# Last batch handed from experts to routing on chip, the experts' deadline moved by 19 turns, and expert places counted by running sums

## The chip, the cores and the metric

The kernel runs on one core of a Trainium2 chip. A core has five engines with a queue of instructions each: TensorE (PE; its weight loads are listed as PEld), VectorE (DVE), ScalarE (ACT), GpSimd (POOL) and SyncE (SP), which here issues nearly all the ordinary DMAs; GpSimd issues the indirect ones. The metric is the device time of one execution in microseconds; the number compared is the median of several runs.

## What is computed

The reference is two transformer layers over 16 batches of 512 tokens with 128 features, all in float32. Cut to what matters here:

```
xn = layernorm(x)
x  = x + memory_scan(xn) + L0(xn)       # L0: conv, attention, layernorm, 8 dense experts, layernorm
xn = layernorm(x)
x  = x + L1_attention(xn) + L1_experts(xn)

# end of L0, after the dense experts
x1 = x1 + moe_out;  L0 = layernorm(x1) * g2 + b2n

# L1_attention: causal attention, a convolution, causal attention again, a projection
# L1_experts: 32 experts, the best 8 for each token, at most 128 tokens for each expert
logits = xn @ gate.T;  top 8;  softmax weights
pos  = cumsum(one_hot(expert), axis=0) - 1        # place of a token in its expert's buffer
buf  = zeros(E, 128, H).at[expert, pos].set(xn)   # places from 128 on are dropped
eo   = (silu(buf @ gate_w) * (buf @ up_w)) @ down_w
out  = sum over the token's 8 experts of eo[expert, pos] * weight
```

The cumulative sum runs over all tokens of all batches, so no expert's list of tokens is known before the last batch has been routed.

## The kernel before

**Turns.** The program is a set of Python generators (stages), and the class Turns steps each of them once in a turn, in order of a priority number. What a stage emits between two yields lands in the engines' queues in that place. TensorE's order is exactly the order written; 1275 turns make the program. A stage can wait for a mark that another has set (after), for some turns (idle) or for a free PSUM bank (room).

**What runs in them.** For each batch of layer 0: front0, tops and back (attention), post0, then ffn (the 8 dense experts: 32 pieces, each one first, the matmul pair phe, and one second, the four calls into pye; the result of an expert is scaled by ScalarE into y and added to ac by GpSimd, L618). For each batch of layer 1: middle (layernorm after the experts, residual sum into acc, layernorm, router, and a table ctab of running counts inside each tile of 128 tokens), front1, tops and back twice with between, and last. Layer-1 batches start 44 turns apart (TBB) from turn 480 (t0). tops writes scores s and takes their row maxima on VectorE (L395, or L402 and L403); these go through DRAM back into rows of qx (top, L420 and L424); back computes s again, exp on ScalarE into e (L475), masks the diagonal block on GpSimd (L483), or on VectorE once the gathers are over (L481), and multiplies with the values into pc.

**How the dense experts are spread.** ffn takes in each turn as many pieces as a credit allows; the credit grows by due(b, left), which spreads all pieces still to do evenly over the turns up to pools["until"]. At the end of each turn fill adds a dummy matmul (L206) when the turn holds little work for TensorE and no dense-expert piece was handed out in the last turns.

**The last batch.** ffn stores its result ac to DRAM (x1d); middle loads it two idle turns ahead of its use, computes both layernorms (VectorE the moments, GpSimd the rest), stores the transposed xT to DRAM (xt), and front1 loads it again and waits three turns.

**Places.** route (here the end of middle) copies, for each tile of 128 tokens, each expert's total into a column of totT by a DMA of 0.1 KB (L1235). When the last batch is routed and all weight tiles lent from the pool mid are read, the stage moe begins. It loads the mask memE, makes running sums of the 64 columns of totT in six doubling steps on VectorE (L1337, L1338), spreads them over partitions by four matmuls pt (512 columns each, from a masked product bd), and finds for each expert and place the tile (istar) and the place in it (base). 32 indirect gathers gt from ctab (L1375) and counts lt (L1369) give the tokens. Then 16 pairs of experts follow, three turns apart: gather the tokens xg (L1413), transpose (tpx), pgu, peo, and scatter-add eo into acc in DRAM (L1458). At the end total adds what attention left in ao for the last batches and writes out (L1485, L1492).

Of the kernel before, what the change touches and what calls it, by code (L numbers as in the profile page):

```python
# [82 lines left out]
def network(ctx: ExitStack, tc: tile.TileContext, a, out):  # L83
# [60 lines left out]
    def mark(*m):  # L144
        done[m] = clock[0]
# [375 lines left out]
    credit, fetched = [0.0], {}  # L521
# [24 lines left out]
    def ffn(b):  # L546
# [99 lines left out]
        nc.sync.dma_start(x1d[0, b], flat(ac))  # L646
# [536 lines left out]

    def middle(mid, b):

        yield from after(("ffn", b))
# [20 lines left out]
        yield from idle(2)  # L1207
        yield from room()
# [34 lines left out]
        mark("xw", b)  # L1243
        yield


    def front1(b):
        yield from after(("x2", b))
        got = []
        yield from take(free_values, got)  # L1250
        z = live[1, b] = {"vp": got[0]}
        xT = l1.tile([P, S], F32, tag="st", bufs=2, name="xT")
        nc.sync.dma_start(xT, xt[1, b])
        yield from idle(3)
# [74 lines left out]
    def moe(mo):  # L1329

        memE = load(mo, "mske", [EXP1, EXP1])

        cur = totT
        s_ = 1
        while s_ < NTILE:
            nxt = mo.tile([EXP1, NTILE], F32, tag=f"cum{s_}", bufs=1, name=f"cum{s_}")
            nc.vector.tensor_copy(nxt[:, 0:s_], cur[:, 0:s_])  # L1337
            nc.vector.tensor_tensor(nxt[:, s_:], cur[:, s_:], cur[:, : NTILE - s_], ALU.add)  # L1338
            cur, s_ = nxt, 2 * s_
        per = 512 // NTILE  # L1340

        def places(u):
# [3 lines left out]
            nc.vector.tensor_tensor(bd, bc(cur, 1, per), bc(memE[:, es], 2, NTILE), ALU.mult)  # L1346
            yield
# [12 lines left out]
        yield from side(*[places(u) for u in range(EXP1 // per)])  # L1360
        nc.vector.tensor_scalar(base, base, -1.0, col("iota"), ALU.mult, ALU.add)
        rowf = mo.tile([P, EXP1], F32, tag="rowf", bufs=1, name="rowf")
# [4 lines left out]
        def count(e):  # L1367
            lt = mo.tile([P, P], F32, tag="lt", name="lt")
            nc.vector.tensor_scalar(  # L1369
                lt, gts[e], base[:, e : e + 1], None, ALU.is_le, ALU.add, accum_out=tok[:, e : e + 1]  # L1370
            )

        for e in range(EXP1):
            gt = mo.tile([P, P], F32, tag="gt", bufs=12, name="gt")
            nc.gpsimd.indirect_dma_start(  # L1375
                out=gt, out_offset=None, in_=ctab,
                in_offset=bass.IndirectOffsetOnAxis(ap=rowi[:, e : e + 1], axis=0),
                bounds_check=EXP1 * NTILE - 1, oob_is_err=True,
            )
# [11 lines left out]
        gidf = mo.tile([P, EXP1], F32, tag="gidf", bufs=1, name="gidf")  # L1391
        nc.vector.tensor_scalar(gidf, tok, float(N - 1), None, ALU.min)
        gidx = mo.tile([P, EXP1], I32, tag="gidx", bufs=1, name="gidx")
        nc.vector.tensor_copy(gidx, gidf)

        inv = mo.tile([P, EXP1], F32, tag="inv", bufs=1, name="inv")
        nc.vector.tensor_scalar(inv, tok, float(N), col("iota"), ALU.is_ge, ALU.mult)
        nc.vector.scalar_tensor_tensor(inv, tok, float(N), inv, ALU.min, ALU.add)
        sidx = mo.tile([P, EXP1], I32, tag="sidx", bufs=1, name="sidx")
        nc.vector.tensor_copy(sidx, inv)  # L1400
        yield

# [94 lines left out]
    pools["until"] = t0 + (B - 1) * TBB - 10  # L1497
# [14 lines left out]
    with tc.tile_pool(name="mid", bufs=1) as mid:  # L1512
# [129 lines left out]
```

## Time and profile before

| | us |
|---|---|
| median of 3 runs | 3590.16 (3588.07 to 3597.58) |
| the profiled execution | 3586.38 |
| its span, first to last instruction | 3584.7 |
| TensorE busy | 3388.3 (95%) |
| VectorE busy | 2319.8 (65%) |
| ScalarE busy | 2217.0 (62%) |
| GpSimd busy | 1541.4 (43%) |

Times below are in us from the start of the span. Because TensorE follows the written order, each turn has a place in the trace, the start of its first matmul:

| turn | starts at | what stands there |
|---|---|---|
| 481 | 1474.0 | layer 1 begins |
| 1131 | 3201.8 | |
| 1133 | 3205.4 | last matmul of the dense experts |
| 1154 | 3252.7 | |
| 1159 | 3262.5 | transposes of the last batch's x2 (tp) |
| 1161 | 3270.0 | |
| 1169 | 3287.1 | first pt |
| 1177 | 3320.1 | first gather is issued to GpSimd's queue (it runs at 3326.5) |
| 1200 | 3379.5 | gathers are over |
| 1210 | 3402.1 | first scatter-add is issued |
| 1258 | 3548.3 | last scatter-add is issued |

A line of a view of waits reads: who waited, for whom, us in total, times, the longest. A line of a timeline has start, length, engine, line, operation, names, and in brackets the engine's idle time before it and what ended that.

### The profile page before, as it was taken

To read this page: it belongs to the slowest core of one execution; us is meant where nothing else is said; L and a number is where in the kernel's file an instruction comes from. 1 tells how busy PE (TensorE), PEld (TensorE's weight loads), DVE (VectorE), ACT (ScalarE), POOL (GpSimd) and SP (SyncE) were. 2 spreads that over 40 slices of the span, in tenths; PEclk is the share of its full clock that TensorE was granted. 3 is DMA by queue.
4 is the path that set the end of the run, shared out by engine and by line. 5 is a ranking of instruction groups with operands and counts; after the bars stand their busy time and mean duration, and the time that the engine had idled before them with its cause. 6 is when DMAs were issued, how large, how long until landed. Compare 5 with 4: busy or idle time off the path is not lost.

```text
span 3584.7 us, 63937 instructions
## 1 busy us (share of the span) xinstructions
PE 3388.3 (95%) x22085; PEld 1903.2 (53%) x22085; DVE 2319.8 (65%) x6045; ACT 2217.0 (62%) x4919; POOL 1541.4 (43%) x2386
## 2 busy tenths in 40 slices
PE   6999999899999999999999999999999999998887
PEld 3445555454555455555555555555555555553444
DVE  5676666566756565556467676666666666667885
ACT  1566656665666787766656666666666666664444
POOL 5423532433531455433544444434444444433653
PEclk7999999899999999999999999999999999998997
DMA  5222222212222233334344444444344434433343
GB/s 176 70 70 71 74 72 78 67 53 85 76 73 88 89 110 108 110 118 125 106 111 136 126 121 113 121 136 122 95 132 121 134 114 111 132 106 98 92 102 91
DMA packets 289794, 370.37 MB, mean 103 GB/s; under 512 B 45984, under 2 KB 141376, under 8 KB 289088
## 3 DMA queue, kind: packets, MB, share of 16 engines
q1 hardware_dynamic: 282304, 359.46, 34.7%
q0 software_dynamic: 7168, 6.82, 1.2%
q8 instruction: 177, 2.90, 0.3%
q14 instruction: 145, 1.19, 0.1%
HBM read 236.58 MB, written 132.99 MB: 103 GB/s over the span
## 4 chain that ended last, share of the span: by engine, by line
PE 50%; DVE 4%; DMA 2%; ACT 2%; POOL 1%; issue 1%; SPq 1%; POOLq 0%; DVEq 0%; ACTq 0%
PE s L197 13%; PE pye L610 10%; PE phe L197 10%; PE pc L197 8%; PE pq L197 1%; DVE s L395 1%; PE fill L206 1%; PE tpc L251 1%; PE tp L251 1%; DVE nm L403 1%; PE po L197 1%; DVE s L402 1%; ACT e L475 1%; PE pjk L197 1%; PE pv L197 1%
## 5 line engine op out<-in xcount | busy, mean ns | idle before, releaser
L475 ACT ACTIVATE e<-s 128x512 f32<-128x512 f32 (+1 forms) x2432 | 1274.6, 576 | 556.6 <-PE s L197 514.3
L403 DVE TENSOR_REDUCE nm<-s 128x1 f32<-128x512 f32 (+2 forms) x1408 | 906.7, 682 | 512.0 <-PE s L197 510.6
L395 DVE CUSTOM_DVE_ANT_0 s<-s,sb_const 128x512 f32<-128x512 f32 (+1 forms) x1024 | 623.4, 643 | 388.2 <-PE s L197 386.6
L483 POOL TENSOR_SCALAR_AFFINE_SELECT e<-e 128x128 f32<-128x128 f32 (+2 forms) x1270 | 426.7, 344 | 746.6 <-ACT e L475 721.1
L197 PE MATMUL s<-kx,qx 64*128 64x512 f32 (+3 forms) x3072 | 624.4, 431 | 44.4 <-ACT e L475 15.4
L197 PE MATMUL pc<-e,vp 128*32 128x512 f32 (+3 forms) x6144 | 625.8, 506 | 13.4 <-POOL e L483 7.2
L610 PEld LDWEIGHTS pye<-ew,hTe 128*128 128x128 f32 x4096 | 519.8, 193 | 177.9 <-issue 157.6
L197 PEld LDWEIGHTS s<-kx,qx 64*128 64x128 f32 x3072 | 272.8, 187 | 574.4 <-issue 226.6
L610 PE MATMUL pye<-ew,hTe 128*128 128x128 f32 x4096 | 563.0, 281 | 1.5 <-ACT hTe L600 1.4
L197 PE MATMUL s<-qx,kx 64*128 64x512 f32 (+3 forms) x3072 | 536.3, 357 | 26.9 <-DVE nm L403 7.8
L197 PE MATMUL phe<-x1T,ew 128*128 128x512 f32 x1024 | 547.5, 619 | 7.0 <-DMA ew<-in_ew 3.0
L600 ACT ACTIVATE hTe<-phe,sb_cols 128x512 f32<-128x512 f32 x512 | 353.7, 691 | 240.7 <-PE phe L197 238.1
L197 PEld LDWEIGHTS s<-qx,kx 64*128 64x128 f32 x3072 | 305.7, 189 | 78.5 <-ACT e L475 20.4
L618 POOL TENSOR_TENSOR ac<-ac,y 128x512 f32<-128x512 f32 x128 | 163.7, 1279 | 422.6 <-ACT y L617 359.9
L402 DVE TENSOR_TENSOR s<-s,sb_const 128x256 f32<-128x256 f32 (+1 forms) x384 | 181.6, 515 | 190.0 <-PE s L197 157.1
L197 PEld LDWEIGHTS pc<-e,vp 128*32 128x32 f32 x6144 | 150.9, 110 | 238.9 <-issue 174.9
L197 PEld LDWEIGHTS phe<-x1T,ew 128*128 128x128 f32 x1024 | 157.9, 192 | 73.1 <-issue 43.5
L617 ACT ACTIVATE y<-pye,pr 128x128 f32<-128x128 f32 x512 | 146.8, 369 | 31.1 <-PE pye L610 26.9
L395 DVE DVE_READ_ACCUMULATOR2_ANT nm<- 128x1 f32 x1024 | 144.0, 141 | 0.0
L212 POOL TENSOR_SCALAR rs_t<-ss 128x4 f32<-128x4 f32 (+1 forms) x56 | 11.5, 206 | 228.6 <-ACT sq L265 227.3
L1458 POOL DMA_INDIRECT acc<-eo,sidx x32 | 51.6, 1612 | 74.3 <-DVE eo L1452 26.6
L212 POOL TENSOR_SCALAR rs_t<-ln_mv 128x4 f32<-128x4 f32 x64 | 12.7, 198 | 162.5 <-DVE ln_mv L222 159.7
(297 smaller groups left out, 3935.7 us busy)
## 6 DMA issues: line engine op xcount, KB each, us to landing
ew<-in_ew SPq DMA_DIRECT2D x256, 256.0 KB
kx<-rk SPq DMA_DIRECT2D x192, 256.0 KB
qx<-rq SPq DMA_DIRECT2D x128, 256.0 KB
rq<-hi SPq DMA_DIRECT2D x64, 256.0 KB
rq<-lo SPq DMA_DIRECT2D x64, 256.0 KB
rk<-hi SPq DMA_DIRECT2D x64, 256.0 KB
rk<-lo SPq DMA_DIRECT2D x64, 256.0 KB
qx<-r SPq DMA_DIRECT2D x64, 256.0 KB
```

The costliest lines, as they stand in the source:

```text
L197: nc.tensor.matmul(o, lhsT=lhsT, rhs=rhs, start=start, stop=stop)
L251: nc.tensor.transpose(tp[:, t * P : (t + 1) * P], src(t), ident)
L395: newest[0] = nc.vector.tensor_tensor_reduce(out=sv[r][:, 0, :], in0=sv[r][:, 0, :], in1=row["caus"][:, S - n :], scale=1.0, scalar=-BIG, ...
L402: nc.vector.tensor_tensor(dg, dg, bc(row["caus"][:, S - P :], 1, per), ALU.add)
L403: newest[0] = nc.vector.tensor_reduce(nm[:, qt, r, t : t + per], sv[r], AX.X, ALU.max)
L475: nc.scalar.activation(e[:, r, 0 : per * n], s[r], AF.Exp, scale=SCALE)
L483: cleared[0] = nc.gpsimd.affine_select(out=ev[:, r, :, 0:P], in_=ev[:, r, :, 0:P], pattern=[[0, per], [1, P]], compare_op=ALU.is_ge, fill= ...
L600: nc.scalar.activation(hs[i], ph, AF.Relu, bias=col("fb", i))
L610: nc.tensor.matmul(pye[0][:, t, :], lhsT=h[:, t * P : (t + 1) * P], rhs=w2[e][:, f, :], start=(f == 0 and t == 0), stop=(f == 3), skip_gro ...
L617: nc.scalar.mul(y[:, t, :], pye[0][:, t, :], pr[:, t, e : e + 1])
L618: nc.gpsimd.tensor_tensor(ac, ac, y, ALU.add)
L1458: nc.gpsimd.indirect_dma_start(out=acc, out_offset=bass.IndirectOffsetOnAxis(ap=sidx[:, e : e + 1], axis=0), in_=eo[:, i, :], in_offset=No ...
```

## The change

- The last batch's ffn keeps ac in SBUF (final["ac"]) and does not store it. A new stage part, centred, takes the place of the first half of middle for this batch. It loads the residual xa once batch 14 is routed and adds the bias on GpSimd. After the last expert it reads ac, and VectorE does centring, scaling and residual sum in two operations for each tile, and the second layernorm's normalising. xT stays in SBUF and front1 uses it without a load or idle turns.
- pools["until"] goes from 10 turns ahead of t0 + 15 x 44 to 9 turns behind it, so that due spreads the dense experts' pieces over 19 turns more.
- The running sums are made batch by batch at the end of route: three turns behind the mark xw, four small VectorE operations on the batch's four columns of totT add to the sums so far, upto. The doubling steps go, and memE is loaded early.
- moe begins as soon as the last batch's sums are marked, in the pool fb, and does not wait for the lent tiles before its pairs. Each of its four places parts has two idle turns between bd and pt, and they start two turns apart. Gather tiles gt have 10 buffers and not 12.

```diff
-        nc.sync.dma_start(x1d[0, b], flat(ac))
+        if b == B - 1:
+            final["ac"] = ac
+        else:
+            nc.sync.dma_start(x1d[0, b], flat(ac))
...
+    def centred(mid, b):
+
+        yield from after(("xw", b - 1))
+        xa = mid.tile([P, TB, D], F32, tag="st", bufs=4, name="xa")
+        nc.sync.dma_start(xa, acc_b[b])
+        yield from idle(3)
+        nc.gpsimd.tensor_tensor(xa, xa, bc(row["b2n"], 1, TB), ALU.add)
+        yield from after(("ffn", b))
+        ac = final["ac"]
...
+        yield from moments(ac, got)
+        mv, rs = got[0]
+        for t in range(TB):
+            nc.vector.scalar_tensor_tensor(
+                x2[:, t, :], ac[:, t, :], mv[:, t, 0:1], row["g2"], ALU.subtract, ALU.mult
+            )
+            nc.vector.scalar_tensor_tensor(
+                x2[:, t, :], x2[:, t, :], rs[:, t : t + 1], xa[:, t, :], ALU.mult, ALU.add
+            )
+            if t == 1:
+                yield
+        yield
+        nc.sync.dma_start(acc_b[b], x2)
+        yield from layernorm(xwt[:, :, 0:D], x2, on=(nc.vector,))
+        yield from room()
+        xT = l1.tile([P, S], F32, tag="st", bufs=2, name="xT")
+        transpose_tokens(xT, xwt[:, :, 0:D])
+        final["xT"] = xT
...
         mark("xw", b)
+        yield from idle(3)
+        of = totT[:, b * TB : (b + 1) * TB]
+        ups = sm.tile([EXP1, TB], F32, tag="ups", name="ups")
+        nc.vector.tensor_copy(ups[:, 0:1], of[:, 0:1])
+        nc.vector.tensor_tensor(ups[:, 1:], of[:, 1:], of[:, : TB - 1], ALU.add)
+        to = upto[:, b * TB : (b + 1) * TB]
+        carry = upto[:, b * TB - 1 : b * TB] if b else 0.0
+        nc.vector.tensor_scalar(to[:, 0:2], ups[:, 0:2], carry, None, ALU.add)
+        nc.vector.scalar_tensor_tensor(to[:, 2:], ups[:, 2:], carry, ups[:, 0:2], ALU.add, ALU.add)
+        mark("upto", b)
...
-        xT = l1.tile([P, S], F32, tag="st", bufs=2, name="xT")
-        nc.sync.dma_start(xT, xt[1, b])
-        yield from idle(3)
+        xT = final.pop("xT", None)
+        if xT is None:
+            xT = l1.tile([P, S], F32, tag="st", bufs=2, name="xT")
+            nc.sync.dma_start(xT, xt[1, b])
+            yield from idle(3)
...
-        memE = load(mo, "mske", [EXP1, EXP1])
-
-        cur = totT
-        s_ = 1
-        while s_ < NTILE:
-            nxt = mo.tile([EXP1, NTILE], F32, tag=f"cum{s_}", bufs=1, name=f"cum{s_}")
-            nc.vector.tensor_copy(nxt[:, 0:s_], cur[:, 0:s_])
-            nc.vector.tensor_tensor(nxt[:, s_:], cur[:, s_:], cur[:, : NTILE - s_], ALU.add)
-            cur, s_ = nxt, 2 * s_
+    upto = mw.tile([EXP1, NTILE], F32, name="upto")
+    memE = load(mw, "mske", [EXP1, EXP1])
+
+    def moe():
+
+        yield from after(("upto", B - 1))
...
-            nc.vector.tensor_tensor(bd, bc(cur, 1, per), bc(memE[:, es], 2, NTILE), ALU.mult)
-            yield
+            nc.vector.tensor_tensor(bd, bc(upto, 1, per), bc(memE[:, es], 2, NTILE), ALU.mult)
+            yield from idle(2)
...
-        yield from side(*[places(u) for u in range(EXP1 // per)])
+        yield from timed(*[(2 * u, places(u)) for u in range(EXP1 // per)])
...
-            gt = mo.tile([P, P], F32, tag="gt", bufs=12, name="gt")
+            gt = fb.tile([P, P], F32, tag="gt", bufs=10, name="gt")
...
+        while "mo" not in pools:
+            yield
+        mo = pools["mo"]
...
-    pools["until"] = t0 + (B - 1) * TBB - 10
+    pools["until"] = t0 + (B - 1) * TBB + 9
...
-        pools.update(weights=[att, fb])
+        pools.update(weights=[att, fb], work=2)
+        turns.stages.append((turns.turn, 3, moe()))
         turns.run(until=lambda: not lent)
     with tc.tile_pool(name="mo", bufs=2) as mo:
-        pools["work"] = 2
-        turns.stages.append((turns.turn, 3, moe(mo)))
+        pools["mo"] = mo
         turns.stages += [(turns.turn, 5, total(b)) for b in range(B)]
```

More of the change, by code (lines that the diff above doesn't have):

```diff
@@ L518, in conv @@
         mm(o[:, 0 : S - 1], w(2), src[:, 1:S], start=False)
-    credit, fetched = [0.0], {}
+    credit, fetched, final = [0.0], {}, {}
     def due(b, left):
@@ L1182, in network @@
     pools["pairs"] = True
+    def centred(mid, b):
[6 more added lines that the diff above has]
+        ac = final["ac"]
+        x2 = mid.tile([P, TB, D], F32, tag="st", bufs=4, name="x2")
+        xwt = mid.tile([P, TB, XW], F32, tag="xwt", bufs=1, name="xwt")
+        got = []
+        yield from moments(ac, got)
[16 more added lines that the diff above has]
+        final["xT"] = xT
+        mark("x2", b)
+        yield
+        return xT, xwt
     def middle(mid, b):
+        if b == B - 1:
+            yield from route(mid, b, *(yield from centred(mid, b)))
+            return
         yield from after(("ffn", b))
@@ L1207, in middle, with route @@
         yield from idle(2)
+        yield from route(mid, b, xT, xwt)
+    def route(mid, b, xT, xwt):
         yield from room()
@@ L1327, in network @@
     tok = mw.tile([P, EXP1], F32, name="tok")
-    def moe(mo):
-        memE = load(mo, "mske", [EXP1, EXP1])
-        cur = totT
-        s_ = 1
-        while s_ < NTILE:
-            nxt = mo.tile([EXP1, NTILE], F32, tag=f"cum{s_}", bufs=1, name=f"cum{s_}")
-            nc.vector.tensor_copy(nxt[:, 0:s_], cur[:, 0:s_])
-            nc.vector.tensor_tensor(nxt[:, s_:], cur[:, s_:], cur[:, : NTILE - s_], ALU.add)
-            cur, s_ = nxt, 2 * s_
+    upto = mw.tile([EXP1, NTILE], F32, name="upto")
+    memE = load(mw, "mske", [EXP1, EXP1])
+    def moe():
+        yield from after(("upto", B - 1))
         per = 512 // NTILE
@@ L1359, in places @@
             nc.vector.tensor_reduce(base[:, es], le, AX.X, ALU.max)
-        yield from side(*[places(u) for u in range(EXP1 // per)])
+        yield from timed(*[(2 * u, places(u)) for u in range(EXP1 // per)])
         nc.vector.tensor_scalar(base, base, -1.0, col("iota"), ALU.mult, ALU.add)
-        rowf = mo.tile([P, EXP1], F32, tag="rowf", bufs=1, name="rowf")
+        rowf = fb.tile([P, EXP1], F32, tag="rowf", bufs=1, name="rowf")
         nc.vector.scalar_tensor_tensor(rowf, istar, float(NTILE - 1), C1("eoff"), ALU.min, ALU.add)
@@ L1367, in count @@
         def count(e):
-            lt = mo.tile([P, P], F32, tag="lt", name="lt")
+            lt = fb.tile([P, P], F32, tag="lt", bufs=2, name="lt")
             nc.vector.tensor_scalar(
@@ L1390, in moe @@
         nc.vector.scalar_tensor_tensor(tok, istar, float(P), tok, ALU.mult, ALU.add)
-        gidf = mo.tile([P, EXP1], F32, tag="gidf", bufs=1, name="gidf")
+        gidf = fb.tile([P, EXP1], F32, tag="gidf", bufs=1, name="gidf")
         nc.vector.tensor_scalar(gidf, tok, float(N - 1), None, ALU.min)
-        gidx = mo.tile([P, EXP1], I32, tag="gidx", bufs=1, name="gidx")
+        gidx = fb.tile([P, EXP1], I32, tag="gidx", bufs=1, name="gidx")
         nc.vector.tensor_copy(gidx, gidf)
-        inv = mo.tile([P, EXP1], F32, tag="inv", bufs=1, name="inv")
+        inv = fb.tile([P, EXP1], F32, tag="inv", bufs=1, name="inv")
         nc.vector.tensor_scalar(inv, tok, float(N), col("iota"), ALU.is_ge, ALU.mult)
         nc.vector.scalar_tensor_tensor(inv, tok, float(N), inv, ALU.min, ALU.add)
-        sidx = mo.tile([P, EXP1], I32, tag="sidx", bufs=1, name="sidx")
+        sidx = fb.tile([P, EXP1], I32, tag="sidx", bufs=1, name="sidx")
         nc.vector.tensor_copy(sidx, inv)
         yield
+        while "mo" not in pools:
+            yield
+        mo = pools["mo"]
         def fetch(e2):
```

## The prediction

> **What bounds the kernel now.** I read the windows first, then TensorE's waits, then GpSimd's timeline at the end. Columns of a window: its length, busy us and instructions of PE, PEld, DVE, ACT and POOL, granted clock, DMA share, GB/s.
>
> ```profile
> 1800.00:3060.00 1260.00, 1244.01 (x9168) 736.38 (x9164) 846.02 (x2594) 814.37 (x1719) 562.63 (x1205) 1.00 0.42 120
> 3201.80:3252.80 51.00, 46.47 (x329) 22.32 (x325) 36.70 (x112) 27.63 (x58) 24.22 (x56) 0.97 0.39 97
> 3218.10:3260.80 42.70, 41.25 (x277) 18.50 (x276) 33.80 (x105) 22.42 (x46) 24.44 (x54) 0.98 0.26 69
> 3297.30:3326.50 29.20, 25.45 (x125) 11.65 (x125) 26.06 (x62) 10.12 (x21) 6.87 (x19) 0.70 0.36 91
> 3326.50:3379.50 53.00, 45.44 (x276) 19.17 (x274) 39.56 (x148) 22.73 (x46) 44.88 (x69) 0.94 0.41 103
> 3405.00:3555.00 150.00, 127.69 (x867) 72.43 (x866) 111.67 (x358) 72.88 (x157) 81.05 (x58) 0.85 0.38 78
> ```
>
> The first row is the long stretch in which layer-0 experts (phe, pye) share the turns with layer-1 attention: TensorE is busy 1244 of 1260 us at clock 1.00, VectorE only 846. It waits for almost nothing there; the three longest entries:
>
> ```profile
> PE phe L197 <- DMA ew<-in_ew: 3.0, 1, 3.0
> PE s L197 <- DMA qx<-top: 2.3, 5, 1.1
> PE tpc L251 <- ACT cs L448: 1.9, 4, 0.5
> ```
>
> So there a turn lasts as long as its matmuls, and a matmul taken out shortens it. After the experts end (3207) it is otherwise: dummy matmuls (fill) pad TensorE, and places that wait stand out. The largest, with the DMA behind it:
>
> ```profile
> PE pt L197 <- DVE bd L1346: 6.3, 1, 6.3
> ```
> ```profile
> 3287.11 0.56 SPq L1235 DMA_DIRECT2D totT<-ct  x1
> ...
> 3291.35 0.14 DVE L1337 COPY cum<-totT 32x1 f32<-32x1 f32 x1 [2.61 <-DMA totT<-ct]
> ```
>
> The last totT copy is issued at 3287.11, VectorE waits until 3291.35, runs twelve small cum operations, and pt starts at 3295.28. From the first gather on, GpSimd's queue sets the pace:
>
> ```profile
> 3326.54 1.34 POOL L1375 DMA_INDIRECT gt<-ctab,rowi  x1 [0.70 <-DMA acc<-xs]
> ...
> 3378.44 1.01 POOL L1375 DMA_INDIRECT gt<-ctab,rowi  x1 [0.30 <-DVE lt L1369]
> 3383.76 1.03 POOL L1413 DMA_INDIRECT xg<-xw,gidx  x1 [2.28 <-DVE gidx L1394]
> ...
> 3404.95 1.68 POOL L1458 DMA_INDIRECT acc<-eo,sidx  x1 [13.33 <-DVE eo L1452]
> ...
> 3474.31 1.57 POOL L1458 DMA_INDIRECT acc<-eo,sidx  x1 [2.45 <-DVE e L481]
> ...
> 3483.06 1.69 POOL L1458 DMA_INDIRECT acc<-eo,sidx  x1 [2.47 <-DVE nm L395]
> ...
> 3553.53 1.55 POOL L1458 DMA_INDIRECT acc<-eo,sidx  x1 [2.45 <-DVE e L481]
> ```
>
> 32 gathers fill 53 us between masks (idle 0.2 to 0.3 before each); 32 scatters follow, one after another's landing, never under 8.75 us a pair (3474.31 to 3483.06); the span ends 31.2 us after the last scatter (3584.7 - 3553.5). So first gather to end is 258.2 us of one queue, and what sets the end is how early the first gather is.
>
> **The change, by turns.** TensorE's order is written out turn by turn, so both programs can be counted; times of turns are those of their first matmul in the trace. Last expert matmul: turn 1133 before, 1151 after. First pt: 1169, then 1174. First gather: 1177, then 1183. Scatters: 1210 to 1258, then 1216 to 1262. Turns in all: 1275, then 1274. Up to turn 1131 (3201.8 us) nothing differs on TensorE but where expert pieces stand and a few small pieces of batch 14's routing.
>
> (a) **Experts taken out of turns 481 to 1130.** Twelve phe (two matmuls each) and thirteen pye groups (eight each) leave. The chain of waits has runs of them at 0.86 and 0.89 us, others at 1.05 and 1.09. 12 x 0.86 + 13 x 0.89 = 21.9, upper end 12 x 1.05 + 13 x 1.09 = 26.8. Cover: none, TensorE is full. Fitting the lengths of turns 568 to 1095 (one attention phase apart) to their expert time gives 0.96 to 1.1 us for each us taken out, 0.79 at the low end of its error: lower end 17. I take -21.9, by the packed rows.
>
> (b) **The same pieces put into turns 1131 to 1153.** These took 51.0 us, with 46.47 busy, so 4.5 idle; twelve fills worth 8.2 us by width (1.05 us for a full one) go, because their room is used. 21.9 - 8.2 - 4.5 = +9.2. At matmul pitch (0.43 us for 512 columns) instead of modelled ends the idle time is 9.5: +4 is the low end. Allowing idle time to be filled only within its own turn gives +12.
>
> (c) **Last expert to first gather.** From turn 1161 (3270.0) to the first gather: 56.5 us before, 16 turns and 6.4 us of queue. After: 22 turns. The unburdened rate is 42.70 us for 20 turns, 2.13 each: 22 x 2.13 + 6.4 = 53.3. The other limit is VectorE: 33.80 / 20 = 1.69 a turn, 37 in all; places 13.7 (four times five operations, 0.67 to 0.75 each, as L1346 to L1359 have them); routing, row splits and values of this batch about 6: 57. Saved: the 6.3 us wait and the 1.8 us of cum operations. Between 53 and 62 (all that and lag), nearest the VectorE sum: 0, ends -4 and +6. The new two-turn gap between bd and pt covers bd's 0.67 us; uncovered, it is four times that.
>
> A row on the clock: after the wait for bd the granted clock is 0.70 for 29.2 us, 8.8 us of array time. The Trainium skill ("TensorE: Matmul & The Clock Gate", "What's actually happening") has half rate after an idle window of about 3.4 us and full rate after about as long of sustained work, which would make the loss some 1.7 us by an estimate from that page. By the row the change would win more, by the page little; the sum above takes none of it, VectorE being the limit there.
>
> (d) **First gather to end.** The same 32 gathers and 32 scatters: 258.2 us kept. Ten gather buffers for twelve: count 0 ran at 3337.16, gather 10 (the first that would reuse a buffer) came at 3342.67, so cost 0; uncovered, one landing (2.9 us). Scatters span 46 turns instead of 48, five pairs beside the last, light attention pass; pairs took 148.6 / 15.5 = 9.6 us, the floor is 8.75, so five at the floor give -4, all -13. I take -2, ends -13 and +3. Attention itself ends eleven turns behind the last scatter's turn and stays hidden behind the 31.2 us.
>
> (e) **Last batch on chip.** Out: store and load of ac, store and load of xT (256 KB each), with their idle turns. In: eight scalar_tensor_tensor and four normalising operations 128x128 on VectorE; nearest rows are 0.24 us (128x32) and 0.42 us (128x256), so 12 x 0.28 = 3.4 us, in turns where VectorE is busy 33.80 of 42.70: mostly covered, +1, ends 0 and +3.4. Behind them on VectorE are the s reductions; TensorE has several banks in hand. SP's queue gets four issues fewer; the early acc load is one issue after xw of batch 14, with nobody waiting.
>
> The skill's GPSIMD Engine Reference, "Specifications", speaks against moving this to VectorE: the two engines contend for SBUF when VectorE reads two inputs there. By it the eight two-input operations, about 2 us by an estimate, might hold GpSimd up; by the row GpSimd is busy 24.44 of 42.70 us there and can take it.
>
> (f) **Running sums.** Four small operations a batch, 64 in all at 0.14 to 0.2, some 11 us of VectorE over 1700 us with a third idle: 0. The new wait, each batch: the operations stand three turns behind xw, the last totT issue is 5 to 6 us behind that turn's start and lands 4.2 later (3287.11 to 3291.35), and VectorE gets there 10 to 12 us behind it: 0.3 to 2.9 us to spare. If that cover is gone, see the second rival.
>
> Sum: -21.9 + 9.2 + 0 - 2 + 1 = -13.7 us. The profiled execution took 3586.4 (span 3584.7): 3572.7. The runs' median is 3590.2, 3.8 more, so the forecast for a median is 3576.
>
> **Rivals.**
> 1. *VectorE takes back the gain before the first gather* (chance 0.27). For it: 26.06 of 29.2 us busy among the places. If twelve of the 22 turns last as those did (29.2 us for 9.6 turns, 3.04): 12 x 3.04 + 10 x 2.13 + 6.4 = 64.2, +8 against 56.5, and 3584. Against: that stretch also had the halved clock and four bd jammed behind a stall.
> 2. *The running sums wait for totT in every batch* (0.08). VectorE is in order: the s reductions stand behind it, and TensorE behind those. For it: the slack of 0.3 us in some batches, and 2.6 us waited before. Sixteen times 2.6 + 0.7 is 53 us: up to 3629; it cancels the forecast from 0.9 us a batch, and makes the kernel slower by over 0.3% from 1.5. Likeliest size 2 us: 3608. Against: VectorE idles 414 of 1260 us.
> 3. *Scatters at their floor and clock kept* (0.07): -13 in (d) for -2: 3565.
>
> **How the numbers follow.** Forecast 0.58, spread 3566 to 3583. A measurement tells about 0.3% (10.8 us, 3579.4) from no change. Faster: 0.50 of the forecast, rival 3, and 0.06 of rival 1: 0.63. Same: 0.08 and 0.21: 0.29. Slower: rival 2, 0.08. The range 3562 to 3589 leaves rival 2 and the ends of the others out.
>
> **What would show it.** Right: turn 1131's matmuls about 22 us earlier (near 3180), 9 of it given back by 1154; no wait of 6 us before pt; first gather near 3315, gather to end 255 to 258. Wrong: matmuls up to 3180 not earlier (then (a) fails), DVE waits for totT in every batch (rival 2), first gather at 3320 or later with VectorE full (rival 1).

## The result, and the profile after

The changed kernel takes 3615.73 us (median of 6 runs, 3612.3 to 3620.25); the kernel before, run beside it, 3590.18 (6 runs, 3588.07 to 3597.58). The ratio is 1.0067, 95% interval 1.0054 to 1.0080: 0.7% slower, where the forecast had 13.7 us faster. The profiled execution took 3620.25 us, span 3618.5. It is the slowest of its six, and the profiled one of the kernel before (3586.38) lies below all six of that kernel: the medians are 25.6 us apart, the two spans 33.9.

The windows of both kernels, cut at the same turns: 481 to 1131, 1131 to 1161, 1161 to the first gather. Columns: the window and its length, busy us and instructions of PE, PEld, DVE, ACT and POOL, granted clock, DMA share, GB/s. First the kernel before:

```profile
1474.00:3201.80 1727.80, 1699.45 (x12193) 995.39 (x12192) 1116.04 (x3362) 1116.97 (x2350) 748.44 (x1517) 1.00 0.42 120
3201.80:3270.00 68.20, 61.43 (x429) 29.31 (x425) 46.75 (x145) 36.03 (x74) 33.77 (x76) 0.95 0.34 85
3270.00:3326.50 56.50, 46.20 (x264) 21.93 (x264) 46.82 (x137) 21.88 (x46) 13.28 (x37) 0.78 0.37 105
```

and the changed kernel:

```profile
1476.10:3205.30 1729.20, 1693.96 (x12064) 985.54 (x12063) 1134.00 (x3422) 1107.78 (x2326) 747.39 (x1514) 0.99 0.42 119
3205.30:3281.50 76.20, 72.40 (x531) 40.71 (x527) 49.65 (x154) 45.74 (x97) 28.25 (x67) 0.98 0.32 84
3281.50:3353.90 72.40, 58.02 (x377) 27.46 (x380) 55.96 (x159) 30.29 (x62) 20.02 (x52) 0.91 0.37 95
```

The first window lost 128 matmuls by the written order (24 of phe, 104 of pye; the rows, which count what overlaps a window, have 129) and is 1.4 us longer. TensorE's busy time fell by only 5.5 us: the granted clock went from 1.00 to 0.99, and matmuls at half clock last twice as long (2.05 against 1.02 us for a phe below). The second grew by 8.0 us. The third grew by 15.9 us with 11.8 us more of TensorE's busy time in it: it holds 22 turns instead of 16, and it waits longer. With turn 481 starting 2.1 us later and 6.4 us more from the first gather to the end, the sum is 2.1 + 1.4 + 8.0 + 15.9 + 6.4 = 33.8, the difference of the spans but for rounding.

**In the first window**, TensorE's largest waits for transfers, first in the kernel before, then in the changed kernel (waiting instruction, what ended the wait; us in all, times, longest):

```profile
PE s L197 <- DMA kx<-rk: 4.5, 2, 2.3
PE phe L197 <- DMA ew<-in_ew: 3.0, 1, 3.0
PE s L197 <- DMA qx<-top: 2.3, 5, 1.1
PE pjq L197 <- DMA xT<-xt: 1.3, 2, 1.1
```
```profile
PE pjq L197 <- DMA xT<-xt: 4.6, 3, 2.3
PE phe L197 <- DMA ew<-in_ew: 4.2, 1, 4.2
PE s L197 <- DMA qx<-top: 4.0, 2, 3.7
PE pgt L197 <- DMA x1T<-x1d: 2.1, 1, 2.1
```

The longest single one, on SP's timeline (start, us for the issue) and then TensorE's:

```profile
1930.77 0.60 SPq L372 DMA_DIRECT2D qx<-rq  x1
1934.82 0.33 SPq L372 DMA_DIRECT2D kx<-rk  x1
...
1937.06 0.43 SPq L532 DMA_DIRECT2D ew<-in_ew  x1
```
```profile
1937.91 1.16 PE L610 MATMUL pye<-ew,hTe 128*128 128x128 f32 x8
1943.23 2.05 PE L197 MATMUL phe<-x1T,ew 128*128 128x512 f32 x2 [4.16 <-DMA ew<-in_ew]
```

SP's issues stand in one order. After qx<-rq SP issues nothing for some 3.5 us (its next, kx<-rk, waits 2.7 us of them for the landing of rk<-lo), then come the rest of the attention's rows, and only then the second expert's weights; TensorE has nothing else in its written order and waits 4.16 us. The phe behind it takes 2.05 us for two matmuls that take 1.02 elsewhere: half clock. The longer deadline moves the boundaries between the experts' batches against the attention's 44 turns, and this one fell on a group of rows. The kernel before with the new deadline alone (e1, below) has the same wait, 4.16 us too.

**In the third window**, TensorE, then VectorE, then SP in the changed kernel:

```profile
3311.30 1.12 PE L206 MATMUL fill<-sb_pd,sb_const 128*128 128x512 f32 x2
3319.53 0.76 PE L197 MATMUL s<-kx,qx 64*128 64x512 f32 x1 [7.10 <-DMA qx<-zrow]
3323.05 0.76 PE L197 MATMUL s<-kx,qx 64*128 64x512 f32 x1 [2.76 <-DMA qx<-zrow]
...
3324.06 3.64 PE L197 MATMUL pc<-e,vp 128*32 128x512 f32 x16
3327.63 1.17 PE L197 MATMUL pt<-bd,sb_const 32*128 32x512 f32 x2
```
```profile
3314.66 0.67 DVE L1397 TENSOR_TENSOR bd<-upto,sb_mske 32x512 f32<-32x512 f32 x1
```
```profile
3307.17 0.80 SPq L338 DMA_DIRECT2D rk<-lo  x2
...
3313.47 0.53 SPq L372 DMA_DIRECT2D qx<-rq  x1
...
3316.07 0.29 SPq L376 DMA_DIRECT2D qx<-zrow  x1
```

The input of the first pt is ready at 3315.33 (3314.66 + 0.67). But ahead of pt on TensorE's queue stand the first scores of the last batch, whose rows SP issues last at 3316.07; they wait 7.10 and 2.76 us, the values (pc) behind them run at half clock, and pt starts 12.3 us after it could have. So the wait for bd that the change removed (6.3 us) came back as a longer one for rows, in the same place.

**At the end**, GpSimd's first gather and the last of its 32 scatters:

```profile
3353.92 1.34 POOL L1426 DMA_INDIRECT gt<-ctab,rowi  x1 [2.38 <-DVE rowi L1415]
...
3587.16 1.63 POOL L1513 DMA_INDIRECT acc<-eo,sidx  x1 [2.35 <-DVE e L481]
```

Gathers again take 53 us, the scatters 154.1 instead of 148.6, and 31.4 us lie behind the last one as before (31.1).

### The profile page after: what moved, and what is told of

Same layout as the page of the kernel before. It is cut to its first block, busy times and chain, and to the rows that moved or that the text cites. A ratio compares the mean times of both kernels' runs of the same rounds, so it can differ in the third digit from the quotient of the medians.

```text
span 3618.5 us, 63994 instructions
## 1 busy us (share of the span) xinstructions
PE 3396.0 (94%) x22069; PEld 1901.6 (53%) x22069; DVE 2338.1 (65%) x6095; ACT 2217.6 (61%) x4919; POOL 1543.7 (43%) x2390
## 3 DMA queue, kind: packets, MB, share of 16 engines
q1 hardware_dynamic: 281728, 358.41, 34.7%
## 5 line engine op out<-in xcount | busy, mean ns | idle before, releaser
L483 POOL TENSOR_SCALAR_AFFINE_SELECT e<-e 128x128 f32<-128x128 f32 (+2 forms) x1284 | 436.3, 349 | 775.8 <-ACT e L475 748.9
L197 PE MATMUL s<-kx,qx 64*128 64x512 f32 (+3 forms) x3072 | 627.4, 430 | 56.0 <-ACT e L475 15.9
L197 PE MATMUL pc<-e,vp 128*32 128x512 f32 (+3 forms) x6144 | 631.0, 504 | 18.9 <-DVE e L481 7.4
L610 PE MATMUL pye<-ew,hTe 128*128 128x128 f32 x4096 | 572.1, 284 | 0.0
L1513 POOL DMA_INDIRECT acc<-eo,sidx x32 | 52.1, 1628 | 78.8 <-DVE eo L1507 37.7
```

Of the source, the lines that this page charges most:

```text
L197: nc.tensor.matmul(o, lhsT=lhsT, rhs=rhs, start=start, stop=stop)
L483: cleared[0] = nc.gpsimd.affine_select(out=ev[:, r, :, 0:P], in_=ev[:, r, :, 0:P], pattern=[[0, per], [1, P]], compare_op=ALU.is_ge, fill= ...
L610: nc.tensor.matmul(pye[0][:, t, :], lhsT=h[:, t * P : (t + 1) * P], rhs=w2[e][:, f, :], start=(f == 0 and t == 0), stop=(f == 3), skip_gro ...
L1513: nc.gpsimd.indirect_dma_start(out=acc, out_offset=bass.IndirectOffsetOnAxis(ap=sidx[:, e : e + 1], axis=0), in_=eo[:, i, :], in_offset=No ...
```

## The experiments

Each ran beside the kernel before on its chip; ratios are to that kernel. "Work" in what follows is the matmuls of turns 481 to 1130, counted from the written order at their pitch when back to back; "idle" the sum of TensorE's waits there; "half clock" the time at half the granted clock. In every kernel the stretch is work + idle + half of the half-clock time + 109 to 114 us, so the three say where a microsecond is. From 1 to 5 us of half clock fall into waits, where they cost nothing. With these left out, the stretch less idle less half of the half clock is 1691.5 to 1691.8 us in the four kernels with the old deadline, and 1670.6 to 1672.2 in the nine with the new one and no added dummy matmuls. So the removed work did come out, some 20 us of it, and all that hides it is waits and half clock. The edit is against the changed kernel unless said otherwise.

| kernel | work | idle | half clock | 481 to 1131 | 1131 to first gather | first gather to end | ratio, 95% |
|---|---|---|---|---|---|---|---|
| before | 1579.0 | 28.3 | 17.1 | 1727.7 | 124.7 | 258.2 | 1 |
| changed | 1557.6 | 35.2 | 47.8 | 1729.2 | 148.6 | 264.6 | 1.0067 (1.0054 to 1.0080) |
| e1_deadline_only | 1557.6 | 33.6 | 30.7 | 1718.2 | 170.3 | 250.7 | 1.0041 (1.0025 to 1.0057) |
| e2_deadline_back | 1579.0 | 28.9 | 27.3 | 1732.6 | 111.0 | 278.6 | 0.9998 (0.9983 to 1.0013) |
| e3_sums_only | 1579.0 | 28.8 | 23.9 | 1731.6 | 132.9 | 259.4 | 1.0008 (0.9995 to 1.0021) |
| e4_fill_beside | 1597.3 | 25.7 | 20.5 | 1742.5 | 151.2 | 265.0 | 1.0082 (1.0060 to 1.0105) |
| e5_weights_act | 1557.6 | 46.9 | 37.5 | 1736.8 | 149.6 | 263.4 | 1.0077 (1.0061 to 1.0094) |
| e6_tables_act | 1557.6 | 34.3 | 44.4 | 1726.4 | 144.0 | 267.9 | 1.0052 (1.0024 to 1.0079) |
| e7_until0 | 1568.7 | 30.1 | 30.7 | 1724.6 | 113.2 | 274.9 | 0.9968 (0.9955 to 0.9981) |
| e8_until28 | 1537.8 | 37.9 | 34.1 | 1703.8 | 181.6 | 253.2 | 1.0050 (1.0032 to 1.0067) |
| e9_scores_later | 1557.6 | 33.4 | 44.4 | 1726.0 | 137.7 | 256.8 | 1.0010 (0.9990 to 1.0029) |
| e10_masks_dve | 1557.6 | 34.7 | 30.7 | 1720.9 | 153.5 | 264.1 | 1.0062 (1.0040 to 1.0084) |
| e11_no_sums | 1557.6 | 33.3 | 37.5 | 1721.6 | 148.7 | 266.4 | 1.0050 (1.0032 to 1.0067) |
| e12_until0_masks | 1568.7 | 29.8 | 27.3 | 1724.4 | 121.5 | 266.6 | 0.9997 (0.9981 to 1.0012) |
| e13_before_later | 1579.0 | 29.1 | 23.9 | 1732.2 | 131.1 | 298.4 | 1.0095 (1.0079 to 1.0110) |
| e14_until0_later | 1568.7 | 30.4 | 41.0 | 1729.9 | 113.7 | 286.9 | 1.0022 (1.0012 to 1.0033) |
| e15_fetch_early | 1557.6 | 30.8 | 20.5 | 1711.2 | 145.9 | 266.6 | 1.0012 (1.0001 to 1.0022) |
| e16_until0_again | 1568.7 | 30.9 | 17.1 | 1719.9 | 111.6 | 276.8 | 0.9981 (0.9970 to 0.9992) |
| e17_fetch_later | 1557.6 | 31.4 | 20.5 | 1712.1 | 134.9 | 258.4 | 0.9963 (0.9949 to 0.9978) |
| e18_until0_fetch | 1568.7 | 30.4 | 34.1 | 1728.9 | 113.5 | 275.5 | 0.9980 (0.9966 to 0.9994) |

### Which part of the change costs

**e1_deadline_only**, the kernel before with the longer deadline alone:

```
-    pools["until"] = t0 + (B - 1) * TBB - 10
+    pools["until"] = t0 + (B - 1) * TBB + 9
```

> The kernel before with only the deadline moved by 19 turns (until = t0 + 15 x 44 + 9). Theory A (with fewer expert matmuls in a turn TensorE's clock halves for longer and DMA waits open, so the turns 481 to 1130 do not get shorter): those turns take 1722 to 1735 us, as in the changed kernel (1729) and before (1728), with some 40 to 50 us at half clock; the last batch then comes 10 turns later, so the end is later than in the changed kernel: 3620 to 3640. Theory B (the running sums, VectorE's 64 small operations and their place in the queues, eat the gain there): turns 481 to 1130 take 1705 to 1712 and half clock stays under 20 us; the end at 3595 to 3610.

**e2_deadline_back**, the changed kernel with the old deadline (the same line, reversed):

> The changed kernel with the old deadline (until = t0 + 15 x 44 - 10): running sums and the way on chip alone. Theory A: turns 481 to 1130 as before (1726 to 1732, half clock under 25 us), last batch 7 turns earlier than before, gathers over 4 turns earlier: 3570 to 3585. Theory B: turns 481 to 1130 take 1735 to 1750 and the end is at 3600 or later.

**e3_sums_only**, the kernel before with the running sums in place of the six doubling steps (the diff's part in route and in moe):

> The kernel before with only the running sums (upto) in place of the doubling steps, the last batch by way of DRAM, old deadline. Theory A: turns 481 to 1130 as before, 1726 to 1732; counted three turns later than before, the 6 us wait ahead of pt gone: 3583 to 3595. Theory B: 3605 or later.

The sums alone, and the sums with the way on chip, can't be told from the kernel before (1 lies in both intervals). The deadline alone makes the kernel 0.4% slower, and with the other two parts 0.7%. So nothing here is slower without the new deadline, which the forecast had as its main gain. Where it costs is not only the stretch: e1's is 9.5 us shorter than that of the kernel before, but its first gather comes 45.6 us later behind turn 1131. In the changed kernel against e2, the same deadline puts it 37.6 us later.

Of what was expected, e1's stretch (1718.2) lies between the bounds of its two theories; e2's Theory A nearly has the stretch (1732.6) but not the end, which it had 5 us or more ahead of the kernel before; e3's Theory A has the stretch (1731.6).

e2 shows besides that an early first gather needn't be an early end: it comes 111.0 us behind turn 1131 instead of 132.9 in e3, but first gather to end grows from 259.4 to 278.6.

**e4_fill_beside**, dummy matmuls allowed in turns with expert pieces too, to keep the clock up:

```
-        if clock[0] - at_ffn[0] > 2 and n > 0 and held[0] < pools["work"]:
+        if (clock[0] - at_ffn[0] > 2 or clock[0] > 480) and n > 0 and held[0] < pools["work"]:
```

> The changed kernel with dummy matmuls allowed beside the dense experts too (68 more of them in turns 481 to 1130, in turns with little for TensorE). Theory A, if the clock is the cause rather than the DMA waits: half clock in 481 to 1130 falls from 48 us to under 25 and the stretch takes 1715 to 1725 in spite of more matmuls; the end at 3600 to 3610. Theory B, or DMA waits as the cause: the stretch takes 1735 or more, the end 3615 to 3630.

Theory B's stretch. Half clock fell from 47.8 to 20.5 us and idle from 35.2 to 25.7, which is worth 23.2 us; the fills cost 39.7 us of work. Net loss: 1742.5 against 1729.2.

### The deadline, at other lengths

**e7_until0** and **e8_until28**, 10 and 38 turns longer than the kernel before instead of 19 (e7's edit; e8 has + 28):

```
-    pools["until"] = t0 + (B - 1) * TBB + 9
+    pools["until"] = t0 + (B - 1) * TBB
```

> The changed kernel with the experts' deadline moved by 10 turns instead of 19. Theory A (every turn of longer deadline costs, as the stretch does not get shorter by the experts taken out of it): between the deadline as before (1.000) and the change (1.0067), so 1.002 to 1.005. Rival (only the places where the experts' batches end against the attention phases matter, chance for each deadline): outside of that, below 0.999 or above 1.007.

> The changed kernel with the experts' deadline moved by 38 turns instead of 19. Theory A: each turn of delay costs about 0.00035, so 1.010 to 1.016. Rival (chance of the alignment): at or below 1.007. The prediction's own sum, for comparison, has each longer deadline win until experts outlast the stretch: below 0.996.

Theory A fell for both: ten turns make the kernel faster, 38 no slower than 19. Nor is it chance alone. Against the four executions with the old deadline (mean 1731.0), 10.3 us of work less give 6.3 us (four executions of that deadline: 1724.6, 1724.4, 1729.9, 1719.9), and 41.2 less give 27.2 in one execution (some 37.7 of it are expert pieces, the rest other pieces whose turns moved). The work taken out comes off at some 0.6 us for each us, net of the waits and half clock that come with it. At 19 turns it does so least: six executions that load weights as the changed kernel does (changed, e1, e6, e9, e10, e11) have a mean of 1723.7, 7.3 us for 21.4. Behind turn 1131 the longest deadline pays with 181.6 us to the first gather.

**e16_until0_again**, e7 a second time:

> e7_until0 a second time, on another chip perhaps. If a deadline of 10 turns longer beats both kernels, the ratio is again 0.995 to 0.999; if that was chance, 0.999 to 1.003.

Faster than the kernel before again, by 0.2%; the upper end of the interval is 0.9992.

### The loads in the stretch

**e5_weights_act**, the experts' weights loaded from ScalarE's queue:

```
-        nc.sync.dma_start(w1[e], a["ew1"][:, e, :])
+        nc.scalar.dma_start(w1[e], a["ew1"][:, e, :])
...
-        nc.sync.dma_start(w2[e], a["ew2"][:, e])
+        nc.scalar.dma_start(w2[e], a["ew2"][:, e])
```

> The changed kernel, with the loads of the experts' weights issued by ScalarE instead of SP; TensorE's order is the same. Theory A (the gain of the stretch 481 to 1130 is lost where SP's queue, in order, holds a weight or row transfer behind one that waits): the two waits of phe for ew (4.2 and 2.2 us) go, with the half clock behind them, and the stretch shortens from 1729 to 1710-1722 us; ratio to the kernel before 1.000 to 1.004. Rival (the stretch has a floor that transfers or other engines set, so that a wait removed turns up elsewhere): stretch 1726 to 1734, ratio 1.006 to 1.008.

A miss for both theories. phe waits for ew no more, but the scores now wait 11.4 us for top and pgt 4.6 us for x1T; idle rises to 46.9. Whether that is ScalarE held by its issues stays open.

**e15_fetch_early**, still on SP, but the next batch's first weights issued at the start of the last expert:

```
+    soon = {}
...
-        fetched[b] = x1T, {}, {}
-        fetch1(*fetched[b][1:], 0)
-        fetch2(*fetched[b][1:], 0)
+        fetched[b] = x1T, *soon.pop(b, ({}, {}))
+        for fetch, w in zip((fetch1, fetch2), fetched[b][1:]):
+            if 0 not in w:
+                fetch(*fetched[b][1:], 0)
...
+            if e + 1 == EXP0 and f < 2 and ("x1", b + 1) in done:
+                (fetch1, fetch2)[f](*soon.setdefault(b + 1, ({}, {})), 0)
```

> The changed kernel, with the loads of the next batch's first expert weights issued at the last expert's start instead of its end (one expert earlier on SP's queue). TensorE's order is the same. Theory A (part of the 15 us missing from the stretch 481 to 1130 are waits for loads at the ends of the experts' batches): PE idle there falls from 33-35 to 26-30 us, the stretch takes 1710 to 1718 us, ratio 1.002 to 1.005. Rival (the waits are for row transfers that stand on SP's queue wherever the weights are): 1720 to 1730 us, ratio 1.005 to 1.008.

Its stretch, then the load and the phe that waited for it in the changed kernel:

```profile
1481.50:3192.70 1711.20, 1680.42 (x12065) 977.98 (x12064) 1135.74 (x3420) 1107.04 (x2326) 744.62 (x1514) 0.99 0.43 121
```
```profile
1934.14 0.43 SPq L532 DMA_DIRECT2D ew<-in_ew  x1
```
```profile
1940.36 1.05 PE L197 MATMUL phe<-x1T,ew 128*128 128x512 f32 x2
```

With TensorE's order untouched, the stretch is 1711.2 us, 18 less than the changed kernel's and 12.5 less than the mean of the six; against the changed kernel idle falls by 4.4 us and half clock by 27.3. The ratio falls by 0.0055. The 4.16 us wait for ew is gone, as the same load stands 3.7 us nearer to the start of its batch on SP (14.2 us behind turn 641 instead of 17.9), and the 3.71 us wait for top at 2526 is down to 0.98. That this is not one execution's luck shows in the others: all six wait 2.4 to 4.2 us for ew some 460 us behind turn 481 and 2.5 to 3.7 us for top some 1040 us behind it, each time with a spell of half clock of 3.4 to 6.8 us beginning there. Neither e15 nor e17, which has the same loads, has either spell, and their longest wait at these places is 1.4 us. So a good part of what the stretch lost were loads late on SP's queue, and the half clock behind them. Not all: the spell at 2382, which no such wait precedes (last section), went from 10.2 to 3.4 us, and pgt now waits 4.5 us for x1T instead of 2.1.

**e11_no_sums**, the doubling steps back in the changed kernel:

```
-        of = totT[:, b * TB : (b + 1) * TB]
...
-        nc.vector.scalar_tensor_tensor(to[:, 2:], ups[:, 2:], carry, ups[:, 0:2], ALU.add, ALU.add)
...
+        while s_ < NTILE:
+            nxt = fb.tile([EXP1, NTILE], F32, tag=f"cum{s_}", bufs=1, name=f"cum{s_}")
+            nc.vector.tensor_copy(nxt[:, 0:s_], cur[:, 0:s_])
+            nc.vector.tensor_tensor(nxt[:, s_:], cur[:, s_:], cur[:, : NTILE - s_], ALU.add)
+            cur, s_ = nxt, 2 * s_
...
```

> The changed kernel without the running sums: the twelve cum operations stand again before the places. TensorE's order is the same. Theory A (the small operations on VectorE shift it, and with it TensorE: three turns, 821, 873 and 907, are 9.3 us longer with them than in the kernel with the longer deadline alone): turns 481 to 1131 take 1717 to 1722 us instead of 1726 to 1729, the wait of some 6 us before pt is back, ratio 1.003 to 1.006. Rival (those three are half-rate windows of the clock that fall there by chance): 1725 to 1730 us again, ratio 1.006 to 1.009.

The stretch is as Theory A has it, but not for its reason: the first of the three places, turns 821 and 822, is 4.7 us longer than in e1 here too, without the sums, and in e10, with them, it is not. It is a spell of half clock that comes in some executions and not in others. The sums are no cause.

### The wait ahead of pt

**e6_tables_act**, the last batch's tables and totals issued by ScalarE:

```
+            by = nc.scalar if b == B - 1 else nc.sync
-            nc.sync.dma_start(ctab_v[:, b * TB + t, :], of)
-            nc.sync.dma_start(totT[:, b * TB + t : b * TB + t + 1], of[:, P - 1 : P])
+            by.dma_start(ctab_v[:, b * TB + t, :], of)
+            by.dma_start(totT[:, b * TB + t : b * TB + t + 1], of[:, P - 1 : P])
```

> The changed kernel, with the eight small stores and copies of the last batch's counts (ctab, totT) issued by ScalarE instead of SP; TensorE's order is the same. Theory A (the last batch's rows for the first scores, 7.1 and 2.8 us late near 3320, wait behind these eight issues on SP): the gap shrinks to under 4 us, turn 1161 to first gather takes 60 to 67 us instead of 72.4, the ratio falls by 0.002 to 0.003, to about 1.004. Rival (the rows are late because VectorE's split of them is late): the gap stays within 2 us of 9.9 and the ratio at 1.006 to 1.008.

Half a hit: the scores wait 3.3 us (0.5 and 2.9) instead of 9.9, with a 1.5 us wait for a mask ahead of them. But turn 1161 to first gather is still 70.7 us, and pt starts only 2.1 us nearer to tp. Half clock is 13.7 us there in both kernels, but in the changed one 8.2 us of it fall into the waits, here 1.5: the work is slower by half of the other 6.7.

**e9_scores_later**, the scores put behind pt on TensorE's queue instead:

```
-        yield from idle(3)
+        yield from idle(7 if (layer, b, i, c) == (1, B - 1, 0, 0) else 3)
```

> The changed kernel, with the last batch's first scores begun four turns later, so that another attention pass (batch 13's) and the first matmul of the places (pt) stand ahead of them on TensorE; the attention then ends nine turns later. Theory A (in the changed kernel the first pt is ready at 3315.3 but stands on TensorE's queue behind scores that wait for their rows until 3323.1): the gaps of 7.1 and 2.8 us go, the first gather comes 56 to 63 us behind turn 1161 instead of 72.4, the span shortens by 5 to 12 us, ratio 1.003 to 1.005. Rival (first gather to end is not what sets the end, the attention is): the first gather comes earlier, but the end stays or is later, ratio 1.0067 or above.

TensorE's timeline at the first pt of e9:

```profile
3303.32 1.92 PE L197 MATMUL pc<-e,vp 128*32 128x512 f32 x16
3305.84 1.12 PE L197 MATMUL pt<-bd,sb_const 32*128 32x512 f32 x2 [0.59 <-DVE bd L1397]
```

pt waits 0.59 us for its own input and for nothing else; pc is at full clock (1.92 us against 3.64). Turn 1161 to first gather is 63.8 us instead of 72.4, a little more than Theory A had, and the ratio 1.0010, better than it had. Part of that is the end: the scatters take 145.5 us instead of 154.1, in an attention order where batch 13's second pass goes ahead.

**e13_before_later**, the same edit in the kernel before:

> The kernel before, with the last batch's first scores begun four turns later (the same edit as e9_scores_later). Theory A (the wait on rows ahead of pt is a consequence of the change: the kernel before has its first pt wait for bd, not behind those scores): the first gather and the end move by less than 6 us, ratio 0.998 to 1.001. Rival (the order of these scores costs the kernel before just as much, and the edit is a gain of its own): ratio 0.993 to 0.996, and the change's own price stays 0.006.

The distance from the last batch's transposes (tp) to the first pt doesn't move (28.5 us against 28.8), so this wait belongs to the change. The ratio missed both theories: the attention, nine turns longer, now ends late, its scores waiting 20.3 us for top, and 61.7 us lie behind the last scatter instead of 31.1.

**e14_until0_later**, the same edit with e7's deadline:

> The changed kernel with the deadline moved by 10 turns (e7_until0) and the last batch's first scores four turns later. Theory A (the wait on rows costs this deadline too: pt 32 us behind tp there): first gather 5 to 12 us earlier than in e7_until0, ratio 0.990 to 0.995. Rival (attention's end, nine turns later, sets the end): ratio 0.996 to 1.000.

The rival, and beyond it, at 1.0022: last scatter to end 59.6 us. The first gather came no earlier behind turn 1131 (113.7 us, 113.2 in e7).

### Early gathers

**e10_masks_dve** and **e12_until0_masks**, the attention's masks on VectorE from the last routing on, in the changed kernel and in e7:

```
-                    if ("counted",) in done:
+                    if ("upto", B - 1) in done:
```

> The changed kernel, with the attention's masks on VectorE instead of GpSimd from the last routing on (before: from the end of the gathers on). TensorE's order is the same. Theory A (GpSimd's queue from the first gather on sets the end, and the 20 masks between the gathers hold it up): the gathers take 38 to 46 us instead of 52.8, the span shortens by 5 to 12 us, ratio 1.003 to 1.006. Rival (VectorE is full while the places are counted and takes it back): the first gather comes 3 to 8 us later and the ratio stays at 1.006 to 1.008.

> The changed kernel with a deadline of 10 turns longer (e7_until0) and the masks on VectorE from the last routing on. Theory A (in e7_until0 the early gathers stand on GpSimd behind masks that wait for ScalarE, 12.7 us in all, so 64 us for 32 gathers): the gathers take 40 to 50 us, ratio 0.990 to 0.995. Rival (attention's own pace sets the end once the gathers are early): the ratio stays at 0.996 to 0.998 with scatters that wait longer.

What they meant to remove, on GpSimd's timeline of e7:

```profile
3322.81 1.27 POOL L1371 TENSOR_TENSOR xs<-xs,xo 128x512 f32<-128x512 f32 x1
3330.19 0.67 POOL L483 TENSOR_SCALAR_AFFINE_SELECT e<-e 128x128 f32<-128x128 f32 x2 [6.12 <-ACT e L475]
3331.28 1.03 POOL L1426 DMA_INDIRECT gt<-ctab,rowi  x1 [0.42 <-issue]
```

Gathers stand behind masks whose exponentials are not there yet: 6.12 us here, 2.70 us at the next. With the masks gone the 32 gathers take 46.0 us instead of 52.8 in e10, and 52.6 instead of 63.9 in e12. But the time ahead of them grows: first pt to first gather 33.9 instead of 26.3 us in e10, 36.5 instead of 29.1 in e12. The rivals give that to VectorE. In e12 VectorE is indeed full there (busy 35.59 of 36.52 us, 29.00 of 29.07 in e7); in e10 it is busy 29.55 of 33.93 us, 24.40 of 26.29 in the changed kernel, and the granted clock is 0.77 instead of 1.00, which alone makes up nearly all of the 7.6 us: 14.8 us of TensorE's work there are at half clock. That VectorE pays is thus not shown for e10. Neither edit brought the end nearer: e10's ratio (1.0062) is where its rival had it, and e12 takes 388.1 us from turn 1131 to the end, as e7 does, with a ratio (0.9997) above what either theory had.

### Both losses taken out

**e17_fetch_later** has the edits of e15 and e9, **e18_until0_fetch** those of e7 and e15:

> The changed kernel with both edits that won a part back: the weights of the next batch's first expert loaded one expert earlier (e15_fetch_early), and the last batch's first scores four turns later (e9_scores_later). Theory A (two separate losses: load waits and half clock in the stretch, the wait ahead of pt at its end): they add up, stretch 1709 to 1716 us, turn 1161 to first gather 60 to 65 us, ratio 0.994 to 0.998, faster than the kernel before. Rival (one loss seen twice, or attention's later end takes the place): ratio 0.999 to 1.003.

> The changed kernel with the deadline moved by 10 turns (e7_until0) and the early loads of e15_fetch_early. Theory A (the load waits at the ends of the experts' batches cost this deadline as well, idle 30 us): stretch 1708 to 1716 us, ratio 0.991 to 0.996, the fastest here. Rival (these waits were particular to the longer deadline): stretch 1718 to 1726 us, ratio 0.997 to 0.999.

e17's windows, cut at the same turns as above:

```profile
1473.30:3185.40 1712.10, 1680.67 (x12065) 978.37 (x12064) 1134.91 (x3420) 1107.68 (x2326) 745.04 (x1514) 0.99 0.44 121
...
3258.40:3320.30 61.90, 56.90 (x383) 27.66 (x382) 56.35 (x160) 30.27 (x62) 19.99 (x53) 0.97 0.36 96
```

1712.1 and 61.9 us: both within what Theory A had. The two edits gave 0.0055 and 0.0057 alone and 0.0104 together, so the losses are separate. e17 takes 3582.55 us where the kernel before takes 3596.13 beside it; no kernel here has a lower ratio, but e7's (0.9968), with the shorter deadline alone, can't be told from it. e18 is a miss for Theory A: with e7's deadline the early loads give nothing (1728.9 us), so which transfer is late depends on where the boundaries fall. The early loads were not tried in the kernel before, so a part of e17's gain could be had without the change.

## Why the prediction was wrong, step by step

**(a), experts taken out of turns 481 to 1130, failed.** Its size of the work was right: 21.4 us by the count, 21.9 forecast. What failed is "Cover: none, TensorE is full", with a low end of 17. The stretch fell by 7.3 us on the mean of six executions, and not at all in the profiled one. Against the four with the old deadline (idle 28.8, half clock 23.1 us on the mean), these six have 34.1 and 39.3: 5.3 us more waits, and 8.1 from half the extra 16.2 us of half clock, together 13.4 of the missing 14.1. The text read three waits of 3.0, 2.3 and 1.9 us (from 1800 to 3060 alone), called TensorE full, and didn't ask which transfers the moved boundaries would make late. SP's queue was read for the steps at the end, but not here, where 256 KB loads moved past row transfers. With the loads earlier (e15, e17) the stretch is 1711.2 and 1712.1 us: 19.8 and 18.9 us shorter, inside the forecast's bounds. What the same loads would give with the old deadline is not known.

**(b), the pieces put into turns 1131 to 1153, was right:** +10.6 us to turn 1154 for +9.2, within 4 to 12; from there to turn 1161 2.7 us were won, so +8.0 in all.

**(c), last expert to first gather at 0 with ends of -4 and +6, failed:** +15.9. The rate was nearly right: 22 turns at 2.13 and 6.4 us of queue make 53.3. TensorE's waits in the window are 14.4 us in all, the 9.9 among them, and 5.5 us of its work are at half clock; take the waits and half of that work from 72.4, and 55.3 is left (55.1 to 55.4 by the same sum in e6, e9 and e17). What the text left out is what stands ahead of pt on TensorE's own queue. It had said that the wait for bd goes, and did not ask what is late next: rows that SP issues behind four tables and four totals. Rival 1 had the time of the first gather (at 3320 or later) but not the mechanism: VectorE idled 4.7 us just before 3320, ahead of pt. Behind pt it was busy 24.40 of 26.29 us, but the turns there, 1175 to 1182, took 2.26 us each, not the rival's 3.04. e9 settles it by the order alone. With these waits out (e17), the window is 61.9 us, +5.4 and so just inside the ends, with VectorE busy 56.35 us, near the 57 that the text had summed.

**(d), first gather to end, -2 with ends of -13 and +3:** +6.4. The same 53 us of gathers, as said; 46 turns instead of 48 did not make the scatters shorter (154.1 us). GpSimd is busy 80.2 us in that stretch, 79.6 in the kernel before, so what grew are its waits, which turns alone do not set; why they grew stays open. The floor of 8.75 us a pair was a misreading: in the same trace of the kernel before the last pairs come 7.93 to 8.20 us apart. That "what sets the end is how early the first gather is" does not hold in general: a first gather 22 us nearer to turn 1131 (e2 against e3) brought 2.7 us at the end, and later scores in the kernel before made the attention the end (e13).

**(e) and (f):** nothing speaks against them. e2 and e3 can't be told from no change, no wait of VectorE for totT is in the trace, and rival 2, the one that stood for slower, did not happen. Rival 3 did not either. That the slower side would come from (a) and (c) together was in no rival.

**By size**, in the two profiled spans, the forecast missed by 47.5 us (from -13.7 to +33.8): 23.3 in (a), where -21.9 became +1.4, 15.9 in (c), 8.4 in (d), 2.1 ahead of turn 481, less 1.2 in (b) and the 1.0 of (e), which no window shows by itself. That e17 is 13.6 us faster, the size forecast for the change, is luck: it has two edits more.

## What to carry to other kernels

An engine that is 98% busy need not be bound by its work alone: here TensorE was full as long as its loads landed in time, and an edit that moved work about also moved it against those loads. Before counting removed work as gain, list the transfers that the moved work needs and what stands ahead of them on the issuing queue. And when a wait is removed, read the queue of the instruction that waited, from there backwards: the next late thing in front of it takes the wait's place.

## What the runs showed of the hardware

**Half clock costs about half of its time.** Turns 1 to 480 have the same matmuls in all these kernels. In e9's profile they hold 105.8 us of half clock and take 1461.2 us, in e11's 133.1 and 1475.3: 27.3 us more, 14.1 us longer. That is 0.4% of the whole time between two executions of the same matmuls. A line through all 20 profiles gives 0.47 us for each us of half clock.

**It comes in steps, and not in every execution.** All spells of it between turns 481 and 1131 are 3.4, 6.8, 10.2 or 13.7 us long. Most begin within a few us of a wait of over 1 us, at much the same places in the kernels with the same order. Not all: in the changed kernel's profile one of 10.2 us begins at 2382, where TensorE's largest wait in the 10 us before is 0.58 us, and within it TensorE is not idle at all. The same phe and pgt there, first in the changed kernel, then in e1:

```profile
2383.88 3.75 PE L197 MATMUL phe<-x1T,ew 128*128 128x512 f32 x4
2387.42 1.71 PE L197 MATMUL pgt<-sb_gw,x1T 128*128 128x8 f32 x8
```
```profile
2375.46 1.96 PE L197 MATMUL phe<-x1T,ew 128*128 128x512 f32 x4 [0.69 <-DVE nm L403]
2377.25 0.95 PE L197 MATMUL pgt<-sb_gw,x1T 128*128 128x8 f32 x8
```

e1 waits more (0.69 us) and keeps full clock; e6, e9 and e11 have the spell of 10.2 us at this place too, e10 has none. The Trainium skill ("TensorE: Matmul & The Clock Gate", "What's actually happening") describes windows of some 3.4 us that run freely, whatever the kernel does. The steps agree with that, and so may the chance in whether a spell falls at a place. The same section has half rate after an idle window; if that means one without work, this spell does not agree, as no wait of even 1 us stands ahead of it.
